# Block 0's layer 2 of a ternary feed-forward kernel: low parts in float16 against bfloat16 weights, and block 14's omitted low parts restored

## The chip, the cores and the metric

The kernel runs on one core of one Trainium2 chip. The metric is the time of one execution on the device, in microseconds (us). Three runs of the kernel before gave 963.41 (median), 963.37 and 963.62. Line numbers of the form L36 are those of the kernel before.

## The reference

The input x is 128 x 64 x 512 in float32 (batch, channel, feature). What is computed, with the shapes of this case:

```
w  = weights[conditions]                      # 128 x 64 x 64, one matrix for each batch row
c  = einsum('bct,bcd->bdt', x, w)
h  = gelu(c @ tern(W1).T + b1)                # 512 -> 2048 features
y  = h @ tern(W2).T + b2                      # 2048 -> 512 features
s  = max|y| / 7 + 1e-8                        # over the whole tensor
out = x + clip(round(y / s), -7, 7) * s
```

Here tern(W) is alpha * sign(W) where |W| > delta, and 0 elsewhere; delta is 0.05 of the largest |W|, and alpha is the mean of |W| over the entries that are kept. So the weights of both layers are, but for one factor, -1, 0 or 1. The factor is applied afterwards, to the sums.

## The kernel before

**Numbers.** The data are cut into a high part in float32r, the format in which PE multiplies float32 data, and a low part, the remainder. Both are multiplied by the same ternary weights and summed in one accumulator. High parts need the weights in float32r: GpSimd (POOL) makes that copy shortly before its use (CAST wf). Low parts in float16 can use the narrow copy of the weights (bfloat16 or 8 bits). To keep the float16 remainders out of the range of tiny numbers, the blocks 1 to 15 multiply h by 64 (`UP`) before it is cut in two, and divide it out in the factor (`alpha_up`, alpha[3]).

**Blocks.** The 128 batch rows are 16 blocks of 8 rows: 4 pairs (`PAIRS`) of 128 tokens, 512 tokens a block. The 2048 hidden features are 16 chunks (`NH`, index hc) of 128. For each chunk, layer 1 makes a sum of 128 x 512 (ph); ACT turns it into h by Gelu and copies it to the high part; the low part follows; then layer 2 adds the chunk's share to four sums (py, one for each pair), four matmuls for the high part and four for the low part. Blocks 2 to 15 do layer 1 for two chunks at a time by a scheme of seven products in place of eight (the groups named xy and z, function `seven`), and within such a step the layer 2 of the two chunks of the step before (`before[0]`, `before[1]`).

**Block 0** is different, since the ternary weights are made meanwhile by ACT, DVE and POOL. All of its layer 1 comes first: function `early(hc)` gives PE's matmuls, `early_bend(hc)` the Gelu and the cutting in two. In the same loop POOL is given the cast of a coming chunk's weights (`widen1(0, hc + 3)`), and DVE finds W2's threshold and makes its ternary weights (`top`, `junk<-top_w`, `delta_w`, `junk<-nat`, `terns<-nat` in the rows of the profile). The low part is a plain subtraction, 128x512: on POOL for the chunks 0, 2, 4 and 6 (`on_pool`), on DVE for the others, there at places given by calls of `low(0, hc)`. High and low part of block 0 are both float32r and stand in `pairs0`, eight large tiles; both are multiplied by the same float32r copy of the weights (`wide2`, the last expression of the line below). Then comes block 0's layer 2, chunks 0 to 13, with four small groups of block 1's conditioning (pc) in between; chunks 14 and 15 follow within the first steps of block 1.

```
w = wide2[n, hc], wide2[n, hc] if n == 0 else w2t[:, hc]          # L460, layer2
```

**Order.** Each engine takes its instructions in the order of the program: a helper (`InOrder`, L36) records every one, so that all rows of the profile bear this line. What an instruction needs of another engine is a semaphore wait. Tiles come from pools whose slots are used again in turn, and a new tile waits for the last reader of the slot's old one.

**The last blocks.** The output needs the largest |y| of all, so the kernel ends with block 15 and the scaling of what is left. In the first step of block 15 the layer 2 is that of block 14's chunks 14 and 15. There the kernel before leaves out the matmuls of the low parts, by the condition in `seven` at L879: low parts are done only if the block at hand is not the last, or if the chunk is below `HELD` (8). The low parts themselves are computed all the same.

Of the kernel before, what the change touches and what calls it, by code (L numbers as in the profile page):

```python
# [10 lines left out]
F32R = mybir.dt.float32r  # L11
F8 = mybir.dt.float8e4
F16 = mybir.dt.float16
# [3 lines left out]
ALU = mybir.AluOpType  # L17
# [3 lines left out]
P = 128  # L21
# [3 lines left out]
UP = 64.0  # L25
# [14 lines left out]
def tile_cond_ternary_ffn(  # L40
# [12 lines left out]
    pe, act, dve, pool, sp = (  # L53
        InOrder(tc, e) for e in (nc.tensor, nc.scalar, nc.vector, nc.gpsimd, nc.sync)
    )
    B, C, T = x.shape
    S, _, D = weights.shape
    NT = T // P
    NH = W1.shape[1]
    assert 2 * C == P and 2 * D == P and C == D and W1.shape == (P, NH, NT, P)  # L60
    PAIRS = 4
    BLK = PAIRS * P
    NB = B // (2 * PAIRS)
    NG = 4
    GH = NH // NG
    WCH = GH * T
    LAG = 2
    SEVEN = range(2, NB)
    HELD = NH // 2
# [7 lines left out]
    big = ctx.enter_context(tc.tile_pool(name="big", bufs=20))  # L77
# [38 lines left out]
    for g in range(NG):  # L116
        w = big.tile([P, GH, T], F32, tag="big", name=f"nat1_{g}")
# [6 lines left out]
    for g in range(NG):  # L124
        w = big.tile([P, GH, T], F32, tag="big", name=f"nat2_{g}")
        sp.dma_start(out=w, in_=W2[:, g * GH : (g + 1) * GH, :])
        nat2.append(w)
    b2b = const.tile([P, T], F32)
# [67 lines left out]
    def split(src, hi, lo, engine=dve):  # L196

        act.copy(hi, src)
        engine.tensor_tensor(lo, src, hi, ALU.subtract)
# [61 lines left out]
    def group1(tiles, g):  # L261
        return tiles[g // 2][:, g % 2, :]
# [99 lines left out]
    wide2 = {}  # L362
    ypsum = {}
    ys = []

    ymax = const.tile([P, NB, PAIRS], F32)
    alpha = {}
# [50 lines left out]
                    stop=(c == NT - 1 and k == 1),  # L418
                )

    def bend(n, hc, ph, two, hf, engine=dve):
        act.activation(hf, ph, AF.Gelu, bias=b1t[:, hc : hc + 1], scale=alpha[1])
        if n > 0:
            up(two[0], hf)
            open_low[n, hc] = lambda: rest(two, hf)
        elif engine is None:
            act.copy(two[0], hf)
            open_low[n, hc] = lambda: dve.tensor_tensor(two[1], hf, two[0], ALU.subtract)
        else:
            split(hf, *two, engine)  # L430
        hidden[n, hc] = two

    open_low = {}
# [14 lines left out]
    def up(high, h):  # L448
        act.activation(high, h, AF.Copy, scale=UP)

    def rest(two, h):
        dve.scalar_tensor_tensor(two[1], h, UP, two[0], ALU.mult, ALU.subtract)

    def low(n, hc):

        open_low.pop((n, hc), lambda: None)()

    def layer2(n, hc, js=range(PAIRS), ks=(1, 0), ends=None):
        two = hidden[n, hc]
        w = wide2[n, hc], wide2[n, hc] if n == 0 else w2t[:, hc]  # L460
        begins, ends = ks[0], ks[-1] if ends is None else ends
        if n not in ypsum:
            ypsum[n] = [
                ps_y.tile([P, T], F32, tag=f"py{j}", name=f"py{j}_{n}") for j in range(PAIRS)
            ]
        for k in ks:
            for j in js:
                pe.matmul(
                    out=ypsum[n][j],
                    lhsT=two[k][:, j * P : (j + 1) * P],  # L470
                    rhs=w[k],
                    start=(hc == 0 and k == begins and ends != begins),
                    stop=(hc == NH - 1 and k == ends),
                    skip_group_check=True,
                )

    def both_layer2(n, hc):
        if n == 0 or hc in (0, NH - 1):
            layer2(n, hc, (0, 1), (1, 0))
            layer2(n, hc, (2, 3), (0, 1))  # L480
        else:
            layer2(n, hc)

    def result(n, j):
        if j == 0:
            ys.append(big.tile([P, PAIRS, T], F32, tag="big", name=f"y{n}"))
        dve.scalar_tensor_tensor(
            ys[n][:, j, :], ypsum[n][j], alpha[2 if n == 0 else 3], b2b, ALU.mult, ALU.add
        )

    def largest(n, j):
# [3 lines left out]


    waiting = {}
    pairs0 = {}
    rings = [half.tile([P, 2, BLK], F32, tag="half", name=f"ring_{i}") for i in range(5)]
    ring = [t[:, i, :] for t in rings for i in range(2)]  # L500
    ring += [quarter.tile([P, BLK], F32, tag="quarter", name=f"ring_{i}") for i in (10, 11)]
# [10 lines left out]
        waiting[hc] = ph  # L512

    def early_bend(hc):
        if hc % 2 == 0:
            pairs0[hc // 2] = big.tile([P, 2, 2, BLK], F32R, tag="big", name=f"h_{hc}")
        two = [pairs0[hc // 2][:, hc % 2, k, :] for k in range(2)]
        on_pool = hc in (0, 2, 4, 6)
        bend(0, hc, waiting.pop(hc), two, ring[hc % len(ring)], pool if on_pool else None)

    def alpha_1():
# [26 lines left out]

    def group2(g):
        return group1(terns2, g)  # L550

    def largest2(g):
        dve.tensor_reduce(
            top_2[:, g : g + 1], flat(nat2[g]), AX.X, ALU.max, apply_absolute_value=True
        )
# [120 lines left out]
        behind(hc)  # L676
    for hc in range(NH - 4, NH):
        early_bend(hc)
    for hc in (5, 7, 8, 9):
        low(0, hc)  # L680

    w1t = big.tile([P, NH, T], F8, tag="big", name="w1t")
# [6 lines left out]
    for hc in range(NH - LAG):  # L689
# [10 lines left out]
        if hc == 4:  # L700
            two_next = parts(1)
            w2t = big.tile([P, NH, T], F8, tag="big", name="w2t")
        if hc in (5, 7, 9, 11):
            j = (hc - 5) // 2
# [12 lines left out]
    hf = ring[:2]  # L717
# [11 lines left out]
    def sums_of(k):  # L729

        if not sums:
            for i in range(2):
                sums.append(half.tile([P, NH // 4, 4, 2 * P], F8, tag="half", name=f"sums_{i}"))
        return [sums[k // 4][:, k % 4, i] for i in range(4)]
# [70 lines left out]
    def seven(n, k, behind, before, last):  # L805

        xb, xt, xl = cond[n]
        b11, b21, b22 = [(xb[:, i : i + 2], xl[:, i : i + 2]) for i in (0, 2, 4)]
        t1, t2, t3, t4 = [(xt[:, i : i + 2], xl[:, i + 6 : i + 8]) for i in (0, 2, 4, 6)]
        x, y = extra["xy"] if k % 2 == 0 else extra["xy"][::-1]  # L810
        x, y = x[:, :HALF], y[:, :HALF]
        z = extra["z"]
        p4, p5 = z[:, :HALF], z[:, HALF:]

        def both(w, narrow):
            return w, narrow.rearrange("p (c h) -> p c h", c=2)

        s0, s1, s2, s3 = sums_of(k)
        w11, w12 = both(w1f[0][:, :2], a11[:, k]), both(w1f[0][:, 2:], a12[:, k])
        w22 = both(w1f[1][:, 2:], a22[:, k])  # L820
        u0, u1 = both(w1f[1][:, :2], s0), both(w1f[2][:, :2], s1)
        u2, u3 = both(w1f[2][:, 2:], s2), both(w1f[3][:, :2], s3)

        def tokens(t):

            return t.rearrange("p (j h d) -> p h j d", j=PAIRS, h=2)

        def turned(t):
            return t.rearrange("p (j d) -> p j d", j=PAIRS)

        def gelu7(i, h):
            act.activation(h, h, AF.Gelu, bias=b1t[:, 2 * k + i : 2 * k + i + 1], scale=alpha[1])

        def high7(i, h):
            hc = 2 * k + i
            hidden[n, hc] = two = two_of(n, hc)
            up(two[0], h)
            open_low[n, hc] = lambda: rest(two, h)

        ha, hb = hf[0], hf[1]  # L840
        if n == NB - 1 and k % 2 == 1:
            ha, hb = extra["x"][:, 0, :], extra["x"][:, 1, :]
        ha_2, hb_2 = tokens(ha), tokens(hb)
        behind(0)
        product(x, w11, b11, 0, first=True)
        product(p5, u0, t1, 0, first=True)
        product(p4, w22, t4, 0)
        product(x, w11, b11, 1, last=True)
        act.copy(ha_2[:, 0], turned(x))
        product(p5, u0, t1, 1, last=True)  # L850
        product(p4, w22, t4, 1, last=True)
        act.copy(hb_2, z.rearrange("p (h j d) -> p h j d", h=2, j=PAIRS))
        behind(1)
        product(y, w12, b21, 1, first=True)
        product(y, w12, b21, 0, last=True)
        dve.tensor_tensor(ha_2[:, 0], turned(y), ha_2[:, 0], ALU.add)
        product(x, u1, t2, 0)
        product(x, u1, t2, 1, last=True)
        act.copy(ha_2[:, 1], turned(x))
        behind(2)  # L860
        product(p5, u2, b22, 1)
        product(p5, u2, b22, 0, last=True)
        dve.tensor_tensor(ha_2[:, 1], turned(p5), ha_2[:, 1], ALU.add)
        behind(3)
        layer2(*before[0], (0, 1), (0,), ends=1)
        product(x, u3, t3, 0)
        product(x, u3, t3, 1, last=True)
        dve.tensor_tensor(
            hb_2, turned(x).unsqueeze(1).to_broadcast([P, 2, PAIRS, C]), hb_2, ALU.add
        )  # L870
        gelu7(0, ha)
        behind(4)
        if last:
            high7(0, ha)
            gelu7(1, hb)
        else:
            gelu7(1, hb)
            high7(0, ha)
        if n < NB - 1 or before[0][1] < HELD:  # L879
            layer2(*before[0], (0, 1), (1,), ends=1)  # L880
            layer2(*before[0], (2, 3), (1,), ends=0)
            layer2(*before[1], ks=(1,), ends=0)
        layer2(*before[0], (2, 3), (0,), ends=0)
        layer2(*before[1], ks=(0,), ends=0)
        high7(1, hb)
        for i in range(2):
            low(n, 2 * k + i)
        behind(6)
# [220 lines left out]
    while s < len(steps):  # L1109
        n, hc = steps[s]  # L1110
# [10 lines left out]
    n = NB - 1  # L1121
# [108 lines left out]
```

## Time and profile before

| what | value |
|---|---|
| median of three runs | 963.41 us |
| the profiled execution's own time | 963.14 us |
| its span, first to last instruction | 961.4 us |
| PE (matmuls) busy | 949.9 us, 99% |
| DVE busy | 708.3 us, 74% |
| POOL busy | 705.3 us, 73% |
| ACT busy | 637.0 us, 66% |
| mean granted clock of TensorE | 0.999 |

A row of a timeline has the start in us from the span's start, the duration, the engine, the line, the operation, the tiles that are written and read, shapes and types, and the count of instructions in the group. In brackets stands the idle time before the group, with what ended it. Groups of PE overlap a little in these rows, since matmuls are pipelined. Block 0's layer 1 lasts until 51.15 us, its layer 2 until 80.40; block 15's first step begins at 896.32, where the group xy<-xb starts.

### The profile page before, as it was taken

The numbers are of one execution on the slowest core, as the hardware profiler recorded it, in microseconds if no ns is written. First come the engines' busy times: TensorE is split into PE (matmuls) and PEld (weight loads), VectorE is DVE, ScalarE is ACT, GpSimd is POOL, SyncE is SP. The second block draws the span as 40 slices with busy tenths as digits, with TensorE's granted clock in tenths as the row PEclk, the third lists the DMA queues.
The fourth block names the chain that finished last, engine by engine and source line by source line (L and its number), as shares of the span: only waits on it lengthen the run. The fifth ranks groups of instructions, "written<-read, shape, count | busy, mean of one in ns | idle before, by whom it ended". The sixth has DMA issues, their size and how long they took to land.

```text
span 961.4 us, 17574 instructions
## 1 busy us (share of the span) xinstructions
PE 949.9 (99%) x6072; PEld 739.3 (77%) x6072; DVE 708.3 (74%) x1239; ACT 637.0 (66%) x1148; POOL 705.3 (73%) x1060
## 2 busy tenths in 40 slices
PE   8999999999999999999999999999999999999997
PEld 4687667888788788788878778788878878878784
DVE  7999766666676766666676676666667798888986
ACT  7995446656656666665666656666565777878784
POOL 6866867677686776767767686776767879788872
PEclk9999999999999999999999999999999999999999
DMA  9301011110111100111010111100131184575751
GB/s 359 103 23 47 14 33 49 32 61 15 35 49 34 60 24 25 52 41 49 25 70 15 34 50 33 59 25 25 49 121 60 47 305 172 186 239 170 277 204 61
DMA packets 33195, 80.11 MB, mean 83 GB/s; under 512 B 3792, under 2 KB 3792, under 8 KB 30160
## 3 DMA queue, kind: packets, MB, share of 16 engines
q1 hardware_dynamic: 31056, 76.86, 22.7%
q0 software_dynamic: 2048, 2.10, 0.7%
q8 instruction: 49, 0.80, 0.3%
q14 instruction: 42, 0.34, 0.1%
HBM read 46.44 MB, written 32.51 MB: 82 GB/s over the span
## 4 chain that ended last, share of the span: by engine, by line
PE 96%; DVE 2%; DMA 1%; ACT 1%; issue 0%; POOL 0%; SPq 0%; ACTq 0%
PE py L36 47%; PE xy L36 22%; PE z L36 16%; PE pc L36 6%; PE ph L36 6%; DVE top L36 1%; DMA nat<-in_L_ffn_W 1%; DVE xt L36 0%; DVE y_last L36 0%; ACT diag L36 0%; POOL wf L36 0%; PE number L36 0%; DVE y L36 0%; ACT h L36 0%; ACT ring L36 0%
## 5 line engine op out<-in xcount | busy, mean ns | idle before, releaser
L36 PE MATMUL py<-wf,h 128*128 128x512 f32 x1088 | 316.5, 416 | 0.7 <-DVE y L36 0.6
L36 POOL CAST wf<-w2t 128x512 fp32r<-128x512 fp8e4 x240 | 229.6, 977 | 105.2 <-PE py L36 102.1
L36 POOL CAST wf<-sums 128x256 fp32r<-128x256 fp8e4 (+1 forms) x336 | 183.0, 550 | 86.1 <-PE xy L36 82.3
L36 PEld LDWEIGHTS py<-wf,h 128*128 128x128 f32 x1088 | 196.6, 189 | 45.1 <-POOL wf L36 0.8
L36 DVE SCALAR_TENSOR_TENSOR low_parts<-ring,h 128x512 f16<-128x512 f32 x228 | 202.1, 924 | 39.3 <-ACT h L36 39.3
L36 PE MATMUL py<-w2t,low_parts 128*128 128x512 fp8e4 x920 | 218.6, 379 | 0.0
L36 ACT ACTIVATE ring<-ring,b1t,alpha_up 128x512 f32<-128x512 f32 x216 | 175.2, 818 | 58.8 <-DVE ring L36 53.9
L36 DVE TENSOR_TENSOR ring<-xy,ring 128x256 f32<-128x256 f32 x216 | 119.8, 555 | 119.3 <-PE xy L36 119.3
L36 ACT COPY ring<-xy 128x256 f32<-128x256 f32 x216 | 80.5, 373 | 171.7 <-PE xy L36 171.2
L36 PEld LDWEIGHTS <-low_parts 128*128 128x128 f16 x920 | 89.6, 97 | 84.5 <-issue 0.3
L36 ACT ACTIVATE h<-ring 128x512 fp32r<-128x512 f32 x232 | 133.9, 626 | 0.6
L36 POOL CAST wf<-w1t 128x256 fp32r<-128x256 fp8e4 (+1 forms) x240 | 131.3, 563 | 2.5 <-PE xy L36 0.3
L36 PE MATMUL xy<-xb,wf 128*128 128x256 f32 x448 | 98.8, 302 | 0.0
L36 PE MATMUL xy<-xt,wf 128*128 128x256 f32 x448 | 88.1, 277 | 0.1
L36 PE MATMUL xy<-xl,sums 128*128 128x256 f16 x448 | 87.9, 278 | 0.0
L36 PE MATMUL xy<-xl,w1t 128*128 128x256 f16 x448 | 86.8, 275 | 0.0
L36 PE MATMUL z<-xl,sums 128*128 128x256 f16 x448 | 85.5, 273 | 0.0
L36 PEld LDWEIGHTS xy<-xt,wf 128*128 128x128 f32 x448 | 76.2, 188 | 10.2 <-issue 0.2
L36 PEld LDWEIGHTS xy<-xb,wf 128*128 128x128 f32 x448 | 75.9, 189 | 10.2
L36 PEld LDWEIGHTS <-sums 128*128 128x128 fp8e4 x896 | 69.3, 97 | 14.8
L36 POOL DMA_INDIRECT wg<-in_L_cond_weights,rows x64 | 63.9, 998 | 18.2 <-issue 8.6
L36 PEld LDWEIGHTS <-w1t 128*128 128x128 fp8e4 x736 | 61.6, 98 | 18.0 <-issue 4.3
(134 smaller groups left out, 1349.3 us busy)
## 6 DMA issues: line engine op xcount, KB each, us to landing
xt<-in_x SPq DMA_DIRECT2D x36, 512.0 KB, 5.6
y_dram<-y SPq DMA_DIRECT2D x15, 1024.0 KB, 4.3
out<-xt SPq DMA_DIRECT2D x30, 512.0 KB, 3.4
x_quarters<-in_x SPq DMA_DIRECT2D x56, 256.0 KB, 2.7
nat<-in_L_ffn_W SPq DMA_DIRECT2D x6, 1024.0 KB, 10.2
y_back<-y_dram SPq DMA_DIRECT2D x2, 1024.0 KB, 7.4
nat<-in_L_ffn_W SPq DMA_DIRECT2D x3, 512.0 KB, 8.7
wg<-in_L_cond_weights,rows POOLq DMA_INDIRECT x64, 2.5
```

What stands on the lines that cost most here:

```text
L36: return lambda *args, **kw: self._tc.keep_in_program_order(make(*args, **kw))
```

## The change

In block 0, h is multiplied by 64 as in the other blocks; its high part stays float32r (`high0`, four tiles), its low part becomes float16 (`low0`, two tiles), and the low part's 64 matmuls take the bfloat16 ternary weights directly (`group2_of`), for the chunks 14 and 15 the 8-bit copy `w2t`. The order within a chunk of block 0 becomes high, low for even chunks and low, high for odd ones. On DVE the low part is one operation, (h * 64) - high. On POOL it is two, a multiplication of h by 64 in place and a subtraction; POOL now has the chunks 0, 2 and 4, and chunk 6 goes to DVE. Block 0's result takes the factor alpha[3]. In block 15's first step the eight matmuls of block 14's low parts are done.

```diff
-    def bend(n, hc, ph, two, hf, engine=dve):
+    def bend(n, hc, ph, two, hf, engine=None):
         act.activation(hf, ph, AF.Gelu, bias=b1t[:, hc : hc + 1], scale=alpha[1])
-        if n > 0:
-            up(two[0], hf)
+        up(two[0], hf)
+        if engine is None:
             open_low[n, hc] = lambda: rest(two, hf)
-        elif engine is None:
-            act.copy(two[0], hf)
-            open_low[n, hc] = lambda: dve.tensor_tensor(two[1], hf, two[0], ALU.subtract)
         else:
-            split(hf, *two, engine)
+            engine.tensor_scalar(hf, hf, UP, None, ALU.mult)
+            engine.tensor_tensor(two[1], hf, two[0], ALU.subtract)
         hidden[n, hc] = two
...
-        w = wide2[n, hc], wide2[n, hc] if n == 0 else w2t[:, hc]
+        w = wide2[n, hc], group2_of(hc) if n == 0 and hc < NH - LAG else w2t[:, hc]
...
     def both_layer2(n, hc):
-        if n == 0 or hc in (0, NH - 1):
+        if n == 0:
+            layer2(n, hc, ks=(0, 1) if hc % 2 == 0 else (1, 0))
+        elif hc in (0, NH - 1):
             layer2(n, hc, (0, 1), (1, 0))
             layer2(n, hc, (2, 3), (0, 1))
...
-            ys[n][:, j, :], ypsum[n][j], alpha[2 if n == 0 else 3], b2b, ALU.mult, ALU.add
+            ys[n][:, j, :], ypsum[n][j], alpha[3], b2b, ALU.mult, ALU.add
...
-        if hc % 2 == 0:
-            pairs0[hc // 2] = big.tile([P, 2, 2, BLK], F32R, tag="big", name=f"h_{hc}")
-        two = [pairs0[hc // 2][:, hc % 2, k, :] for k in range(2)]
-        on_pool = hc in (0, 2, 4, 6)
+        if hc % 4 == 0:
+            high0.append(big.tile([P, 4, BLK], F32R, tag="big", name=f"high0_{hc}"))
+        if hc % 8 == 0:
+            low0.append(big.tile([P, 8, BLK], F16, tag="big", name=f"low0_{hc}"))
+        two = high0[-1][:, hc % 4, :], low0[-1][:, hc % 8, :]
+        on_pool = hc in (0, 2, 4)
...
+    def group2_of(hc):
+        g, i = divmod(hc, GH)
+        return group2(g)[:, i * T : (i + 1) * T]
...
-    for hc in (5, 7, 8, 9):
+    for hc in (5, 6, 7, 8, 9):
         low(0, hc)
...
-        if n < NB - 1 or before[0][1] < HELD:
+        if before[0][0] < NB - 1 or before[0][1] < HELD:
             layer2(*before[0], (0, 1), (1,), ends=1)
             layer2(*before[0], (2, 3), (1,), ends=0)
             layer2(*before[1], ks=(1,), ends=0)
```

More of the change, by code (lines that the diff above doesn't have):

```diff
@@ L497, in tile_cond_ternary_ffn @@
     waiting = {}
-    pairs0 = {}
+    high0, low0 = [], []
     rings = [half.tile([P, 2, BLK], F32, tag="half", name=f"ring_{i}") for i in range(5)]
```

## The prediction

> **What bounds the kernel now.** I read the page's list of engines first, then its chain of work, then the timelines around block 0 and around block 15's first two steps. The page says that TensorE sets the time:
>
> ```profile
> PE 949.9 (99%) x6072; PEld 739.3 (77%) x6072; DVE 708.3 (74%) x1239; ACT 637.0 (66%) x1148; POOL 705.3 (73%) x1060
> PE 96%; DVE 2%; DMA 1%; ACT 1%; issue 0%; POOL 0%; SPq 0%; ACTq 0%
> PE py L36 47%; PE xy L36 22%; PE z L36 16%; PE pc L36 6%; PE ph L36 6%; DVE top L36 1%; DMA nat<-in_L_ffn_W 1%; DVE xt L36 0%; DVE y_last L36 0%; ACT diag L36 0%; POOL wf L36 0%; PE number L36 0%; DVE y L36 0%; ACT h L36 0%; ACT ring L36 0%
> ```
>
> The chain is PE for 96% of the span, and layer 2 (py) is half of it. So two things count: what PE executes, and any new moment at which PE waits. A wait early in the run is not given back, because behind it PE has nearly no idle time left. The profiled execution took 963.14 us, span 961.4 and 1.74 around it; the median of the runs is 0.27 higher, at 963.41. I work out changes of the profiled execution and add them to the median. A measurement of this kernel tells about 0.2% (1.93 us) from no change.
>
> **Part 1, fewer f32 matmuls.** Block 0's 64 low-part matmuls (16 chunks, 4 pairs) become f16. The timeline of PE (start, duration, group) prices both kinds:
>
> ```profile
> 40.21 1.28 PE L36 MATMUL ph<-x,wf 128*128 128x512 f32 x4
> 43.14 0.27 PE L36 MATMUL tops_delta_w<-ident_f,junk 128*128 128x128 f32 x1
> 43.92 1.28 PE L36 MATMUL ph<-x,wf 128*128 128x512 f32 x4
> 45.73 1.28 PE L36 MATMUL ph<-x,wf 128*128 128x512 f32 x4
> 47.54 1.28 PE L36 MATMUL ph<-x,wf 128*128 128x512 f32 x4
> 51.15 11.28 PE L36 MATMUL py<-wf,h 128*128 128x512 f32 x48
> 93.28 1.03 PE L36 MATMUL py<-w2t,low_parts 128*128 128x512 fp8e4 x4
> 893.21 1.89 PE L36 MATMUL py<-w2t,low_parts 128*128 128x512 fp8e4 x8
> ```
>
> A group's duration ends with the drain of its last matmul, so I use differences. f32: (11.28 − 1.28) / 44 = 227.3 ns. f16 data against narrow weights: (1.89 − 1.03) / 4 = 215 ns. So 64 × 12.3 ns = 0.79 us is saved. Against that stand changes of kind: a layer-1 step is four f32 and four f16, lasts 1.81 us (45.73 to 47.54), and its parts make 4 × 0.2273 + 4 × 0.215 = 1.77. One round trip between the kinds costs 0.04. Before, the fourteen chunks between layer 1 and block 1 were f32 throughout; now even chunks run high, low and odd ones low, high, which makes one round trip per two chunks: 7, and one more at chunk 14, whose low parts now stand before block 1's f32 layer 1. 8 × 0.04 = 0.32. **Part 1: −0.47 us** (−0.79 if the changes of kind were free, 0 if an f16 matmul against bf16 weights gained nothing over f32). Weight loads stay hidden: 0.189 us each in f32 and 0.097 in f16, under a matmul of 0.215.
>
> **Part 2, one more POOL operation per chunk, before the weights that layer 1 needs.** POOL copies each chunk's ternary weights to f32 (CAST wf) and, in between, makes low parts. Before, four chunks (0, 2, 4, 6) had one subtraction there. Now three chunks (0, 2, 4) have a multiplication by 64 of 128x512 f32 in place and then the subtraction; chunk 6 moves to DVE. POOL and DVE before:
>
> ```profile
> 36.03 1.29 POOL L36 TENSOR_TENSOR h<-ring,h 128x512 fp32r<-128x512 f32 x1 [0.81 <-ACT h L36]
> 40.50 2.32 POOL L36 TENSOR_TENSOR h<-ring,h 128x512 fp32r<-128x512 f32 x1 [2.06 <-ACT h L36]
> 42.77 1.16 POOL L36 CAST wf<-terns 128x512 fp32r<-128x512 bf16 x2
> 43.90 1.28 POOL L36 TENSOR_TENSOR h<-ring,h 128x512 fp32r<-128x512 f32 x1
> 45.14 1.60 POOL L36 CAST wf<-terns 128x512 fp32r<-128x512 bf16 x1
> 40.47 1.22 DVE L36 TENSOR_TENSOR terns<-masks,signs 128x2048 bf16<-128x2048 bf16 x1
> 41.86 1.05 DVE L36 COPY junk<-top_w 128x128 f32<-128x128 f32 x1
> 44.15 2.12 DVE L36 TENSOR_SCALAR junk<-nat,minus_w 128x2048 bf16<-128x2048 f32 x1
> 46.31 2.58 DVE L36 SCALAR_TENSOR_TENSOR terns<-nat,delta_w,junk 128x2048 bf16<-128x2048 f32 x1
> ```
>
> The reader should see two things. First, the pair of casts at 42.77 is for chunks 12 and 13; chunk 12's ends at 43.38 and PE starts chunk 12 at 43.92, so only half a microsecond is spare, while everything that is added in front of it on POOL (three multiplications, TENSOR_SCALAR) comes to several. Second, POOL and DVE take turns. POOL's subtraction at 40.50 lasts 2.32 instead of 1.29, ending 1.14 after DVE's 40.47 product (41.68). DVE's small COPY lasts 1.05 and ends with it (42.91). DVE's 44.15 operation waits out POOL's to 45.19 and then takes 1.08 to 46.27; POOL's cast of chunk 14 waits in turn until 46.74; DVE's 46.31 starts at work then, 2.15 to 48.89.
>
> The trace has no POOL TENSOR_SCALAR of 128x512. The same operation on shorter rows:
>
> ```profile
> 14.01 1.79 POOL L36 TENSOR_SCALAR diag<-wg 64x256 f32<-64x256 f32 x2 [4.82 <-DMA wg<-in_L_cond_weights,rows]
> 119.18 0.81 POOL L36 TENSOR_SCALAR diag<-wg 64x64 f32<-64x64 f32 x2
> ```
>
> Half of each is 0.90 us for 256 elements and 0.41 for 64: 2.55 ns an element, so another 256 make 1.55. The 256 form writes four pieces of 64, though, so part of this may be a price per piece; the lower bound is a one-input CAST of 128x512, 0.6 (1.16 for two). I take 1.5, from the operation itself, and keep 0.6 to 1.6. The Trainium skill's GPSIMD Engine Reference, section 4.1 Engine selection, says that elementwise work with one input is roughly at line rate on GpSimd and only two inputs are about twice as slow; by that the multiplication would cost about as little as the cast, and part 2 next to nothing. The trace's slope of 2.55 ns speaks against it.
>
> The walk with 1.5, a cast at 0.57 and a subtraction at 1.24 (spacings in the rows above). Chunk 0: multiplied from 33.37, where its subtraction began before, to 34.87, subtracted to 36.11; cast of chunk 9 to 36.7; chunk 2 multiplied to 38.2 and subtracted to 39.44; casts of 10 and 11 to 40.0 and 40.6, the first just in time for PE at 40.21. So far the gaps of 0.81 and 2.06 us, in which POOL waited for ACT, hide it. Chunk 4's multiplication now meets DVE's 40.47 product in the place of the subtraction: it ends 1.5 − 0.15 = 1.35 behind 41.68, at about 43.1. DVE's COPY ends with it, 0.3 late, and with it PE's small matmul at 43.14 and DVE's next large operation, asked for at 44.45 instead of 44.15. Subtraction: 43.1 to 44.39. Cast 12 comes up at 44.35, a tenth before DVE's 44.45, so it goes first and ends at 44.95: PE's chunk 12 starts 1.05 late (this covers the 0.3). DVE's operation to 46.03, cast 13 to 46.6, needed by 45.73 + 1.05: in time. DVE's next runs 46.6 to 48.75, cast 14 behind it to 49.25, needed by 47.54 + 1.05: another 0.66 late. Cast 15 is in time. Total 1.71, less the 0.06 by which chunk 15 waited for its cast before: **part 2: +1.65 us**. From 51 us on PE runs without waits to block 1, so nothing takes it back.
>
> The other pieces of this part cost nothing: ACT's scaled copy replaces a plain one (0.62 each way); chunk 6's low part is one more DVE operation of 0.5 to 1.1 us after 48.8, needed by PE ten microseconds later (if that cover failed, its 1.1 would be the price); two tiles fewer let a load of x start earlier; the result of block 0 takes a factor that is computed one 0.15 us operation later, with PE on other work.
>
> **Part 3, block 14's left-out low parts.** Eight more f16 matmuls, 8 × 0.215 = 1.72 us, in block 15's first step. DVE made these low parts already. PE there, and the DVE operation it waits for:
>
> ```profile
> 900.03 1.63 PE L36 MATMUL py<-wf,h 128*128 128x512 f32 x6
> 905.05 1.07 PE L36 MATMUL py<-wf,h 128*128 128x512 f32 x2 [0.59 <-DVE y L36]
> 904.17 2.71 DVE L36 SCALAR_TENSOR_TENSOR y<-py,alpha_up,b2b 128x512 f32<-128x512 f32 x4
> ```
>
> Block 15's layer 2 may start only when DVE has taken block 14's sums out (y, four at 904.17). DVE comes to that when its queue lets it, behind the first step's low parts, not when PE is done. Steps of PE, from the start of one group xy<-xb to the next: 889.51, 896.32, 901.50, 909.52, 916.62, that is 6.81, 5.18 (the short one), 8.03 (with the wait) and 7.09. Three regular steps would be 20.43, and the three last are 20.30. So the eight matmuls fill the wait: **+0.13 us**, between 0 and 1.72 if y moved back with them.
>
> **Sum**: −0.47 + 1.65 + 0.13 = +1.3 us, 963.41 + 1.3 = 964.7.
>
> **Rivals.** *DVE wins the turn.* The walk has cast 12 ahead of DVE by a tenth of a microsecond, less than I can time. If DVE asks first, it runs 44.45 to 45.47, cast 12 ends at 46.05 (chunk 12 is 2.13 late), DVE's next takes 46.05 to 48.2, cast 13 ends at 48.7 against 47.86 (0.84 more): 2.97 − 0.06 − 0.47 + 0.13 = +2.6, 966.0. This is the other side, slower; it decides once the multiplication takes over 1.2 us, below which cast 12 begins well before 44.15. For it: DVE's 44.15 operation got the turn before the waiting cast of 14 in the trace. *POOL has room.* Multiplication near the cast's 0.6, up to 0.75: chunk 4's ends at 42.2, cast 12 at 44.0, 0.2 late, and cast 14 is late only if DVE gets ahead of cast 13 (0.7). Between −0.1 and +0.5, taking 963.3 to 963.9; without any wait the matmuls' saving alone stays, 963.0. For it the price per piece; against it the slope. *Block 14's matmuls are not absorbed*: +1.6 more, 966.3; against it DVE's idle time, which ends with ACT's h before y. *The change doesn't do what it says*: no case for this, as the weights of the 64 matmuls are plainly the narrow ones; if they ran at f32 speed, +0.5.
>
> **How the numbers follow.** Forecast, the walk with a multiplication of 0.8 to 1.6: 0.48 (963.9 to 965.0). DVE first: 0.33 (965.6 to 966.6). Room on POOL: 0.13. Not absorbed: 0.06. Of the second and fourth, nearly all lies over +1.93: slower 0.37. Faster by 1.93 is out of reach of 0.79 + 0.06 saved; 0.05 for what I overlook. Same 0.58. Range 963.1 to 966.6.
>
> **What would show it.** In the changed profile: POOL TENSOR_SCALAR 128x512, its length (1.5, or 0.7); which of cast 12 and DVE's large TENSOR_SCALAR goes first near 44.4; PE's chunk 12 about 1.05 late (2.1 if DVE is first), layer 2 at 52.9 instead of 51.15; 29.25 us from there to block 1's first ph shrinking to 28.8; no wait for y near 905. It is wrong if layer 2 starts on time, or if another engine's wait appears after 93.

## The result, and the profile after

The changed kernel takes 966.69 us (median of 8 runs, 965.86 to 967.2) against 963.38 (963.24 to 963.62): a ratio of 1.0033, 95% interval 1.0024 to 1.0043. It is slower by 3.3 us; 964.7 was forecast, and the median lies 0.09 above the upper end of the range. The profiled execution took 966.00 us. The runs fall into two groups, around 966.0 and around 966.9; the run "after_again" goes into what parts them.

The page of the changed kernel, first the engines' busy time and then the chain that ended last:

```profile
PE 951.3 (99%) x6080; PEld 733.8 (76%) x6080; DVE 710.0 (74%) x1240; ACT 637.5 (66%) x1148; POOL 707.8 (73%) x1062
PE 94%; POOL 2%; DVE 2%; DMA 1%; issue 0%; ACT 0%; SPq 0%; ACTq 0%; POOLq 0%
```

PE's busy time hardly moved (+1.4 us), while POOL, which had 0% of the chain before, has 2% of it. The timelines of POOL, DVE and PE say where (start, duration, group, idle time before and its end):

```profile
37.00 1.50 POOL L36 TENSOR_SCALAR ring<-ring 128x512 f32<-128x512 f32 x1
38.59 1.30 POOL L36 TENSOR_TENSOR low<-ring,high 128x512 f16<-128x512 f32 x1
39.83 1.18 POOL L36 CAST wf<-terns 128x512 fp32r<-128x512 bf16 x2
40.97 2.46 POOL L36 TENSOR_SCALAR ring<-ring 128x512 f32<-128x512 f32 x1
43.51 1.27 POOL L36 TENSOR_TENSOR low<-ring,high 128x512 f16<-128x512 f32 x1
44.73 1.61 POOL L36 CAST wf<-terns 128x512 fp32r<-128x512 bf16 x1
...
40.68 1.39 DVE L36 TENSOR_TENSOR terns<-masks,signs 128x2048 bf16<-128x2048 bf16 x1
42.25 0.37 DVE L36 COPY junk<-top_w 128x128 f32<-128x128 f32 x1
44.35 1.51 DVE L36 TENSOR_SCALAR junk<-nat,minus_w 128x2048 bf16<-128x2048 f32 x1
45.90 2.58 DVE L36 SCALAR_TENSOR_TENSOR terns<-nat,delta_w,junk 128x2048 bf16<-128x2048 f32 x1
```

```profile
42.23 1.27 PE L36 MATMUL ph<-x,wf 128*128 128x512 f32 x4
46.39 1.20 PE L36 MATMUL ph<-x,wf 128*128 128x512 f32 x4 [1.91 <-POOL wf L36]
49.01 1.19 PE L36 MATMUL ph<-x,wf 128*128 128x512 f32 x4 [0.54 <-POOL wf L36]
50.72 1.27 PE L36 MATMUL ph<-x,wf 128*128 128x512 f32 x4
54.33 1.27 PE L36 MATMUL py<-wf,high 128*128 128x512 f32 x4
83.15 1.08 PE L36 MATMUL ph<-x,wf 128*128 128x512 f32 x4
905.87 0.40 PE L36 MATMUL xy<-xb,wf 128*128 128x256 f32 x2
908.63 0.63 PE L36 MATMUL py<-wf,h 128*128 128x512 f32 x2
```

The undisturbed multiplication takes 1.50 us. POOL's cast for chunk 12 comes up at 44.73, but DVE's large operation, asked for at 44.35, takes the turn, and the cast lasts 1.61. PE starts chunk 12 at 46.39 and chunk 13 at 49.01, with two waits for wf. Layer 2 begins at 54.33 (before 51.15) and block 1 at 83.15 (before 80.40). The first matmuls of block 15's layer 2, at 905.05 before and at 908.63 now, no longer wait for DVE's y.

The balance of the two profiled executions, 966.00 − 963.14 = 2.86: PE's rows from 24 to 39 us, ahead of the new waits, are 0.21 to 0.23 later (a difference of the two executions, in which the first loads landed later); the waits brought 54.33 − 51.15 − 0.21 = +2.97; block 0's layer 2 lasts 28.82 instead of 29.25, −0.43; the stretch from there to block 15, with its last two chunks at the head, −0.09 (2.75 later at its start, 2.66 at its end, 898.98 against 896.32); the three steps around block 14's low parts 20.50 instead of 20.30, +0.20. That is 2.86.

### The profile page after: what moved, and what is told of

Its sections match the earlier page's. It is cut to its first block, busy times and chain, and to the rows that moved or that the text cites. A ratio compares the mean times of both kernels' runs of the same rounds, so it can differ in the third digit from the quotient of the medians.

```text
span 964.2 us, 17578 instructions
## 1 busy us (share of the span) xinstructions
PE 951.3 (99%) x6080; PEld 733.8 (76%) x6080; DVE 710.0 (74%) x1240; ACT 637.5 (66%) x1148; POOL 707.8 (73%) x1062
## 4 chain that ended last, share of the span: by engine, by line
PE 94%; POOL 2%; DVE 2%; DMA 1%; issue 0%; ACT 0%; SPq 0%; ACTq 0%; POOLq 0%
PE py L36 47%; PE xy L36 22%; PE z L36 16%; PE pc L36 6%; PE ph L36 4%; POOL wf L36 1%; DMA nat<-in_L_ffn_W 1%; DVE top L36 1%; POOL ring L36 1%; POOL low L36 0%; DVE xt L36 0%; DVE y_last L36 0%; POOL diag L36 0%; ACT diag L36 0%; SPq L36 0%
## 5 line engine op out<-in xcount | busy, mean ns | idle before, releaser
L36 PE MATMUL py<-wf,h 128*128 128x512 f32 x960 | 285.1, 418 | 0.0
L36 PEld LDWEIGHTS py<-wf,h 128*128 128x128 f32 x960 | 173.0, 189 | 39.1
```

The lines of the kernel that those rows point to most:

```text
L36: return lambda *args, **kw: self._tc.keep_in_program_order(make(*args, **kw))
```

## The experiments

Kernels that ran together shared the runs of the kernel before, whose medians lie between 963.34 and 963.46.

**Are the multiplications the cause?** The first edit takes them out of the changed kernel, the second puts them into the kernel before.

```diff
-            engine.tensor_scalar(hf, hf, UP, None, ALU.mult)      # "no_mul"
             engine.tensor_tensor(two[1], hf, two[0], ALU.subtract)
```

> The changed kernel without its three POOL multiplications by 64; this leaves the low parts of chunks 0, 2 and 4 of block 0 wrongly scaled, and only the time is of interest. Queue theory (the three multiplications of 1.5 us make POOL late, and DVE takes the turn before the cast of chunk 12): POOL then has one operation fewer than before the change, PE has no wait for wf between 40 and 52 us, layer 2 of block 0 starts at about 51.1 to 51.4, and the time is 963.0 to 963.2 us (the matmuls' -0.43 and block 14's +0.15 stay). Rival (the stall comes from what else moved: chunk 6 on DVE, other tiles and so other slots): PE still waits 2 us or more near 44 to 49, and the time stays at 965.5 to 967.

Measured: 963.11 us (963.37 for the kernel before, ratio 0.9999, interval 0.999 to 1.0009). The casts of chunks 12 to 15 are one group on POOL, and PE takes chunks 12 and 13 without a wait (both start 0.67 later than in the kernel before, as do, nearly, PE's rows ahead of them):

```profile
43.45 3.27 POOL L36 CAST wf<-terns 128x512 fp32r<-128x512 bf16 x4
44.59 1.28 PE L36 MATMUL ph<-x,wf 128*128 128x512 f32 x4
46.40 1.28 PE L36 MATMUL ph<-x,wf 128*128 128x512 f32 x4
```

```diff
             act.copy(two[0], hf)       # kernel before, `split` written out: "mul_before"
+            if engine is pool and hc < 6:
+                pool.tensor_scalar(hf, hf, 1.0, None, ALU.mult)
             engine.tensor_tensor(two[1], hf, two[0], ALU.subtract)
```

> The kernel before, with a multiplication by 1.0 in place of 128x512 on POOL in front of the subtractions of chunks 0, 2 and 4, and nothing else changed (chunk 6 keeps its subtraction on POOL). Queue theory: chunk 12 starts on PE about 2.2 us late and chunk 13 another 0.8, as in the changed kernel; time 963.4 + 3.0 = 966.4 us, or up to 967.2 if chunk 6's subtraction between the casts of 13 and 14 makes chunk 14 late too. Rival (the multiplications are hidden, and something else of the change is the cause): 963.4 to 963.7.

Measured: 967.99 us, +4.6 (ratio 1.0049, 1.0036 to 1.0063). Chunks 12 and 13 are late as in the changed kernel (waits of 1.89 and 0.53), and there are two more waits, at chunk 14 and at the start of layer 2:

```profile
51.75 1.20 PE L36 MATMUL ph<-x,wf 128*128 128x512 f32 x4 [0.63 <-POOL wf L36]
55.92 4.37 PE L36 MATMUL py<-wf,h 128*128 128x512 f32 x18 [0.28 <-POOL wf L36]
```

So the multiplications alone make the loss. The expectation was 0.8 us too low even at its upper end: with chunk 6's subtraction left on POOL the lateness ran on into layer 2. That starts at 55.92, which is 4.50 later than in the kernel before (0.27 of a later start of this execution taken off), against 2.97 in the changed kernel. So moving chunk 6 to DVE, which the change does too, is worth about 1.5.

**Does block 14's work hide?**

```diff
-        if n < NB - 1 or before[0][1] < HELD:            # kernel before: "lows14_before"
+        if before[0][0] < NB - 1 or before[0][1] < HELD:
```

> The kernel before, with only the eight matmuls of block 14's low parts added. Absorption theory (they fill the wait for DVE's y near 905 us): +0.1 to +0.25 us, 963.5 to 963.7, and no wait for y. Rival (y moves back with them): +1.5 to +1.7, 964.9 to 965.1, and a wait for y of about 0.6 near 907.

Measured: 963.55 us, 0.18 above the 963.37 of the kernel before. The eight matmuls of 1.72 us cost what the three steps showed, 0.2, and PE's list of waits has none for y any more (0.6 before).

**Added time, or a lost turn?** Three kernels vary how many multiplications there are and where they stand. A theory by which POOL's added time itself is paid for expects a share of the loss for each.

```diff
+            if hc == 4:                 # "mul4_only"; "mul02_only" has: if hc < 4
-            engine.tensor_scalar(hf, hf, UP, None, ALU.mult)
+                engine.tensor_scalar(hf, hf, UP, None, ALU.mult)
```

> The changed kernel with the multiplication on POOL for chunk 4 alone (the low parts of chunks 0 and 2 are left unscaled). Turn theory (what counts is that the cast of chunk 12 comes up after DVE's large operation, which is asked for at 44.35 us): the multiplication of chunk 4 starts near 40.7 and ends near 43.2 behind DVE's product, the subtraction ends at 44.5, DVE goes first all the same, and chunk 12 is about 2.0 late, chunk 13 another 0.6: 965.7 to 966.5 us, nearly the whole loss from one multiplication of 1.5 us. Rival (the loss is the added POOL time, shared out over three multiplications): about a third of 3.3, 964.2.

Measured: 965.86 us, ratio 1.0027 (1.0018 to 1.0037): the one multiplication makes 2.5 of the 3.3, and nearly all of the 2.6 that the changed kernel loses in its faster group of runs (966.0). POOL, DVE and PE:

```profile
40.66 2.52 POOL L36 TENSOR_SCALAR ring<-ring 128x512 f32<-128x512 f32 x1 [2.07 <-ACT high L36]
43.27 1.27 POOL L36 TENSOR_TENSOR low<-ring,high 128x512 f16<-128x512 f32 x1
44.48 1.61 POOL L36 CAST wf<-terns 128x512 fp32r<-128x512 bf16 x1
44.27 1.36 DVE L36 TENSOR_SCALAR junk<-nat,minus_w 128x2048 bf16<-128x2048 f32 x1
46.15 1.20 PE L36 MATMUL ph<-x,wf 128*128 128x512 f32 x4 [1.75 <-POOL wf L36]
```

> The changed kernel with the multiplication on POOL for chunks 0 and 2, not for chunk 4 (whose low part is left unscaled). Turn theory: 3 us are added, but they fall into gaps in which POOL waited for ACT; chunk 4's subtraction ends near 43.1, the casts of 12 and 13 end before 44.35, no wait: 963.0 to 963.4 us. Rival (added POOL time counts): two thirds of 3.3 above, 965.5.

Measured: 963.20 us, no loss (0.9998, 0.9989 to 1.0007), though two multiplications, 3.0 us, stand on POOL:

```profile
41.01 2.26 POOL L36 TENSOR_TENSOR low<-ring,high 128x512 f16<-128x512 f32 x1
43.22 3.28 POOL L36 CAST wf<-terns 128x512 fp32r<-128x512 bf16 x4
44.48 1.55 DVE L36 TENSOR_SCALAR junk<-nat,minus_w 128x2048 bf16<-128x2048 f32 x1
44.25 1.28 PE L36 MATMUL ph<-x,wf 128*128 128x512 f32 x4
46.05 1.28 PE L36 MATMUL ph<-x,wf 128*128 128x512 f32 x4
```

Here the casts come up at 43.22, 1.3 before DVE's 44.48, four of them go through in 3.28, and PE takes chunks 12 and 13 without a wait. The first two multiplications fall into gaps in which POOL waited for ACT; they only used up the room.

```diff
+            def on_pool():              # "mul4_later": run behind the casts of 12 and 13
+                engine.tensor_scalar(hf, hf, UP, None, ALU.mult)
+                engine.tensor_tensor(two[1], hf, two[0], ALU.subtract)
+            if hc == 4: open_low[n, hc] = on_pool
...
     def behind(hc):
+        if hc == 10: low(0, 4)
```

> The changed kernel with chunk 4's multiplication and subtraction moved on POOL's queue behind the casts of chunks 12 and 13; the whole computation stays. Turn theory: both casts end before 43.5, PE has no wait for them; the pair ends near 45.1 and DVE's operation waits behind it, the casts of 14 and 15 come at about 46.7 and 49.4, the last of them up to 0.2 late: 963.1 to 963.6 us. Rival (the POOL time itself has to be paid somewhere before layer 2): 965 or more.

Measured: 965.00 us, ratio 1.0017 (1.0008 to 1.0026): half of the loss is gone, not nearly all. The expectation had the pair end at 45.1. But the subtraction lost its turn to DVE's 44.29, then the cast of chunk 14 lost one to DVE's next, and PE waits there:

```profile
44.29 1.56 DVE L36 TENSOR_SCALAR junk<-nat,minus_w 128x2048 bf16<-128x2048 f32 x1
44.85 2.14 POOL L36 TENSOR_TENSOR low<-ring,high 128x512 f16<-128x512 f32 x1
46.93 2.67 POOL L36 CAST wf<-terns 128x512 fp32r<-128x512 bf16 x1
45.88 3.26 DVE L36 SCALAR_TENSOR_TENSOR terns<-nat,delta_w,junk 128x2048 bf16<-128x2048 f32 x1
49.66 1.19 PE L36 MATMUL ph<-x,wf 128*128 128x512 f32 x4 [1.64 <-POOL wf L36]
```

This is again a lost turn, at another place.

**Chunk 4 to DVE.**

```diff
-        on_pool = hc in (0, 2, 4)       # "pool_0_2"
+        on_pool = hc in (0, 2)
...
-    for hc in (5, 6, 7, 8, 9):
+    for hc in (4, 5, 6, 7, 8, 9):
```

> The changed kernel with only chunks 0 and 2 on POOL; chunk 4's low part is one more DVE operation, in front of chunk 5's. Queue theory: only the backlog of two multiplications stays, the casts of chunks 12 and 13 end before 43 us and wait for nobody, PE waits at most 0.1 us for the cast of chunk 10; layer 2 starts at 51.2 to 51.4 and the time is 963.0 to 963.3, a little under the kernel before. Rival (DVE is the tight engine here, and one more operation of 0.5 to 1.1 us in its queue delays the ternary weights of W2): PE waits for wf or low within block 0's layer 2, 964 or more.

Measured: 963.07 us against 963.37 of the kernel before (ratio 0.9998, 0.9989 to 1.0007: no difference that this comparison tells). The four casts end by 44.5, and of PE's waits for wf only one of 0.3 us is left, at 24 us, which the kernel before has too:

```profile
42.20 2.30 POOL L36 CAST wf<-terns 128x512 fp32r<-128x512 bf16 x4 [1.20 <-DVE top_w L36]
44.12 1.27 PE L36 MATMUL ph<-x,wf 128*128 128x512 f32 x4
```

**What a change between f32 and f16 costs.** Both kernels start from "pool_0_2".

```diff
-            layer2(n, hc, ks=(0, 1) if hc % 2 == 0 else (1, 0))
+            layer2(n, hc, ks=(0, 1))    # "kinds_up"
```

> The kernel with only chunks 0 and 2 on POOL (963.07 us), and high before low in every chunk of block 0, so that layer 2 changes between f32 and f16 once more every two chunks: 8 more round trips. If a round trip costs 0.04 us (the term of the prediction): +0.32, 963.4. If it costs nothing: 963.07.

Measured: 963.46 us, +0.39 for 8 more round trips, 0.05 each. The two kernels ran in different rounds, and no interval parts them, so the rows are worth a look, first "pool_0_2" and then "kinds_up":

```profile
51.34 1.28 PE L36 MATMUL py<-wf,high 128*128 128x512 f32 x4
81.11 1.04 PE L36 MATMUL ph<-x,w1t 128*128 128x512 f16 x4
```

```profile
51.37 1.28 PE L36 MATMUL py<-wf,high 128*128 128x512 f32 x4
81.31 1.04 PE L36 MATMUL ph<-x,w1t 128*128 128x512 f16 x4
```

From layer 2's first matmul to block 1's first f16 group it takes 29.94 us in "kinds_up" and 29.77 in "pool_0_2". That is 0.17 for the 7 more round trips of chunks 0 to 13, 0.02 each. So a round trip costs something between 0.02 and 0.05.

```diff
-            layer2(n, hc, ks=(0, 1) if hc % 2 == 0 else (1, 0))
+            elif hc % 2 == 1:           # "kinds_down", chunks 0 to 13
+                for k in (0, 1) if hc % 4 == 1 else (1, 0):
+                    for c in (hc - 1, hc):
+                        layer2(n, c, ks=(k,), ends=1 - k)
```

> The kernel with only chunks 0 and 2 on POOL, and the chunks 0 to 13 of block 0's layer 2 taken in pairs, the high parts of both and then the low parts of both, the next pair the other way round: 3 or 4 round trips fewer. At 0.04 us each: -0.12 to -0.16, 962.93. If a round trip costs nothing: 963.07. If low or high parts come too late for the new order: above 963.07, with a wait of PE in block 0's layer 2.

Measured: 962.98 us, −0.09, a difference that no interval establishes. As it ran, the high parts of chunks 0 and 1 were left out of the sums, their matmuls not.

**One chunk on POOL.**

```diff
-        on_pool = hc in (0, 2)          # "pool_0"
+        on_pool = hc in (0,)
...
-    for hc in (4, 5, 6, 7, 8, 9):
+    for hc in (2, 4, 5, 6, 7, 8, 9):
```

> The kernel with only chunk 0 on POOL, chunks 2 and 4 on DVE. The cast of chunk 10 is then early, and the last wait for wf (0.25 us between the weight loads, 0.06 of PE's time near 40.5 us) goes: 963.0 us. Rival (DVE's queue is the tight one): one more operation of 0.5 to 1.1 us there delays W2's ternary weights and the low parts, 963.3 or more, with a wait in block 0's layer 2.

Measured: 963.02 us, 0.05 under "pool_0_2". As it ran, chunk 2's low part is taken from a buffer that chunk 14 had already overwritten. DVE's queue bears the operation, but there is next to nothing left to gain by it; the wait for wf of 0.3 us that is still listed is the one at 24 us. Chunk 10's, which showed as 0.23 between the weight loads of "pool_0_2" at 40.48, is gone, as expected.

**The best of these.** "kinds_down" with the sums kept whole:

```diff
+                first, second = (0, 1) if hc % 4 == 1 else (1, 0)
+                for k in (first, second):
+                    for c in (hc - 1, hc):
+                        layer2(n, c, ks=(k,), ends=second)
```

> The candidate to beat both kernels, computing all of it: only chunks 0 and 2 on POOL, and block 0's layer 2 taken in pairs of chunks with three or four changes of kind fewer; the high parts of chunks 0 and 1 are kept, which the run with pairs left out of the sums. Expected: no wait for wf after chunk 10, 962.9 to 963.0 us, about 0.4 under the kernel before and 3.5 under the changed one; 963.07 if the order in pairs brings nothing.

Measured: 962.98 us (11 runs, 962.86 to 963.17), the kernel before 963.46 beside it (963.27 to 964.5). It is 3.7 under the changed kernel, and every one of its runs is under every run of the kernel before; by the interval (0.9994, 0.9985 to 1.0003) that lead of 0.5 is not established.

**The second trace of the changed kernel.**

> The changed kernel once more, for a second trace: its runs lay between 965.86 and 967.2 us, wider than the 0.4 of the kernel before. If the spread comes from the same turns of POOL and DVE falling out differently, the waits for wf between 44 and 53 us differ from those of the first trace (1.91 and 0.54) when the time does; if not, these waits are the same, and the difference lies elsewhere.

Measured: 966.27 us (966.06 to 966.99); the traced execution took 966.97, 0.97 more than the first one. The wait at chunk 12 is the same (1.92). What differs is PE's work behind it. Two groups of PE, then PE by stretches, first in this trace and then in the first one (stretch, its length, PE busy and matmuls, granted clock, DMA share, GB/s):

```profile
47.33 1.51 PE L36 MATMUL ph<-x,terns 128*128 128x512 f16 x4
48.91 2.07 PE L36 MATMUL ph<-x,wf 128*128 128x512 f32 x4
```

```profile
44.00:46.25 2.25, 0.38 (x2) 1.00 0.00 0
46.25:47.50 1.25, 1.21 (x5) 1.00 0.03 7
48.00:51.00 3.00, 2.94 (x7) 0.50 0.00 0
51.25:51.50 0.25, 0.25 (x3) 1.00 0.00 0
```

```profile
49.00:50.00 1.00, 0.99 (x4) 1.00 0.00 0
50.00:51.00 1.00, 1.00 (x6) 1.00 0.00 0
```

From about 47.7 to 51.1 us the granted clock is 0.50, and chunk 13 takes 2.75 instead of 1.71, 1.04 us more. The second branch of the expectation holds: the wait at chunk 12 is the same, and what differs lies behind it. The other runs have no trace, only a mean granted clock. In the eight runs first measured, the five of 966.64 us and more have 0.997, the three of up to 966.08 have 0.998; in the eight of "after_again" it is 0.997 for the three from 966.82 on and 0.998 or 0.999 for the five up to 966.33. So in 8 of 16 runs the clock speaks for such a stretch. In all runs of the kernel before it is 0.998 or 0.999. Three other kernels set limits to this reading. In none of "mul4_only"'s ten runs, with waits of 1.75 and 0.55, is it below 0.998. One of "no_mul"'s eleven, which has no new wait, has 0.996 and 965.64 us. And four of "mul_before"'s five have 0.996 or 0.997, at 967.84, 967.92, 968.07 and 968.58 us, where the fifth has 0.999 and 967.99.

## Why the prediction was wrong in size

**The step that failed** is the order at cast 12: the walk had the cast ask a tenth of a microsecond before DVE's large operation, and in the trace it asks 0.38 behind it (44.73 against 44.35). Both sides of the walk were off. (For a comparison 0.21 is added to its times, since this execution started later.)

- DVE came 0.31 earlier. The walk let DVE's small COPY wait for the multiplication, as it had waited for the subtraction before (1.05 us, to 42.91). In the trace the COPY takes 0.37 and ends at 42.62 while the multiplication is running. So DVE's large operation was not put off to 44.45 but asked for at 44.35, which is 44.15 plus the later start. Why the COPY waits for the one and not for the other, no run shows.
- POOL came 0.17 later. Chunk 4's multiplication was to end at 43.1 (43.03 by its own terms, 41.68 + 1.35) and the cast to come up at 44.35; in the trace it is 43.43 and 44.73. DVE's product, behind which the multiplication had to wait, lasted 1.39 instead of 1.22 and ended at 42.07. It had met the casts of chunks 10 and 11, which the first two multiplications had pushed back and which ended at 41.01. In "mul4_only" and "no_mul", where nothing pushes them, the product takes 1.22.

Each of the two alone is more than the tenth on which the walk stood: with DVE at 44.66, where the walk had it, it would still have been 0.07 ahead of the cast. "mul4_only" had the two 0.21 apart, also with DVE first.

From there the rival "DVE wins the turn" is what happened. It named chunk 12 2.13 late and chunk 13 0.84 more, 2.97, of which 2.91 is left behind chunk 15. The trace has 2.26 and 0.81, of which 2.97 is left at the start of layer 2. That both come to 966.0 is in part luck: the rival's sum stands on the median of 963.41, the execution's on 963.14 and a start that was 0.21 later. Its turning point, a multiplication of 1.2 us, fits the gaps at 44.4: 1.5 less 0.21 or 0.38 gives 1.3 or 1.1. This is worked out and was not run.

**The steps that held.** The multiplication at 1.50 was taken as 1.5: the slope of 2.55 ns an element was that of the operation and not a price per piece. The Trainium skill's GPSIMD Engine Reference, section 4.1, which puts one input roughly at line rate, is not borne out for this operation: with one input it cost 1.50 us where the subtraction with two costs 1.29 and the one-input cast 0.6. Part 1 was −0.47, measured −0.43 − 0.09 = −0.52; its price of 0.04 for a round trip lies within the 0.02 to 0.05 measured. Part 3 was +0.13, measured 0.20 in the trace and 0.18 alone. That the first two multiplications hide in POOL's gaps was shown by "mul02_only". The other pieces cost nothing, as said: "no_mul" leaves the change at 963.11.

**What the sum lacked** is the clock. A term for PE running slower behind a new wait was not in it. The turns explain 966.0; that the median is 966.69 comes of the five runs of eight with the lower mean clock, for which one trace shows the stretch of 0.50.

That the turn goes to whoever asks first agrees with the Trainium skill's page SBUF — State Buffer, section "Who interferes with whom": DVE in a two-port mode and GpSimd share a port pair, whoever issues first holds it for the whole instruction, and the other is fully blocked. In the traces DVE asked 0.38 and 0.21 ahead and went first, and in "mul02_only" POOL's casts were 1.3 ahead and did. That DVE goes first whenever both are waiting would fit these rows as well; no run tells the two rules apart. Nor do the runs show which port it is.

## What to carry to other kernels

Where two engines take turns at a resource, price an added operation by whom it lets go ahead, not by its length: here 3 us of work cost nothing in front of a gap, and 1.5 us cost 2.5 by losing one turn and, through it, a second. Before walking such a queue by hand, look in the trace at each pair of operations that is assumed to block, since a multiplication did not hold up the copy that a subtraction of the same size had held up. Put work that is needed late (low parts that layer 2 takes ten microseconds on) on an engine whose queue has no urgent load behind it.

## What the runs showed of the hardware

A wait of PE may cost more than its length. In one of two traced executions of the changed kernel, PE had a granted clock of 0.50 for about 3.4 us, starting 1.4 us after it had resumed work from a wait of 1.92 us (2.41 between the weight loads), and lost 1.0 us by it; in the other, with a wait of 1.91, the clock stayed at 1.00. By their mean clocks 8 of 16 runs had such a stretch. That the wait is what brings it on is likely but not shown, as the run of "no_mul" without one tells. The Trainium skill's page TensorE: Matmul & The Clock Gate, Part 1, tells of a gate that looks at activity in a free-running window of about 3.4 us, grants half or all of the clock, and throttles after an idle window. The half clock, the stretch of 3.4 us and the chance from run to run agree; that less than 2.5 us of idle time came before it, and not a whole idle window, is what this trace adds.

A multiplication of 128x512 in f32 by a constant took POOL 1.50 us, longer than a subtraction of two such tiles (1.29).
